# The last batch norm, residual and layer norm of a four-layer graph network in a written order: normalising on ScalarE, half of the residuals on TensorE, stores by GpSimd

## The chip, the cores and the metric

The kernel runs on one core of one Trainium2 chip. The metric is the device time of one execution in microseconds (us), the median of several runs. Engines: PE is TensorE's matmul, PEld its weight load, DVE is VectorE, ACT is ScalarE, POOL is GpSimd, SP is SyncE. A difference below 2% counts as "the same".

## The reference, cut to what matters

Four layers, each `x = layernorm(x + gnn_layer(x))`, on 128 batches of 128 nodes by 256 features. The change touches only the end of the last one:

```python
def _layernorm(x, axis=-1, eps=1e-5):
    m = jnp.mean(x, axis=axis, keepdims=True)
    v = jnp.var(x, axis=axis, keepdims=True)
    return (x - m) / jnp.sqrt(v + eps)

# layer 3
    x = agg.reshape(-1, d)
    h = jax.nn.relu(_batchnorm(x @ W1.T + b1, g1, be1))
    out = h @ W2.T + b2                  # "z product" below
    out = _batchnorm(out, g2, be2)       # "n2": needs all batches first
    return out.reshape(b, n, -1)
# ... cut
x = _layernorm(x + _L3_gnn_ref(x, adj, ...), axis=-1)   # "last part" below
```

A batch norm needs the moments of every batch, so the end falls into two stages with a full stop between them: the z product (with the first batch norm and relu applied on the way), then n2, the residual `x3` (the input of layer 3), the layer norm and the store.

## The kernel before

A group `q` is four batches (`QB`), and there are 32 groups (`NQ`). The result of the z product stays in SBUF as `agg`, features on partitions (128 x 512 for each half `o` of the 256 features). The last part scales and shifts it on ScalarE, transposes it on TensorE back to nodes on partitions, and VectorE does everything else.

```python
        for q in range(NQ):
            x3 = wk.tile([P, QB, D], F32, tag="x3", name=f"x3l{q}", bufs=7)
            nc.sync.dma_start(x3, x3_dram[q].rearrange("p (b d) -> p b d", b=QB))
            ag = outs[q]
            for o in range(DC):
                nc.scalar.activation(ag[:, o, :], ag[:, o, :], AF.Identity, bias=sh2[:, o:o + 1],
                                     scale=sc2[:, o:o + 1])
            for j in range(0, QB, 2):
                pt = ps("pt3").rearrange("p (b d) -> p b d", d=D)
                for t in range(2):
                    for o in range(DC):
                        nc.tensor.transpose(pt[:, t, o * P:(o + 1) * P], ag[:, o, (j + t) * N:(j + t + 1) * N], ident)
                nc.vector.tensor_add(x3[:, j:j + 2, :], x3[:, j:j + 2, :], pt)
                layer_norm(wk, x3[:, j:j + 2, :])
            nc.scalar.dma_start(out[q * QB:(q + 1) * QB].rearrange("b n d -> n b d"), x3)
```

`layer_norm` of two batches is, on VectorE, two `bn_stats`, two `bn_aggr`, a reciprocal and two `tensor_scalar` (subtract the mean, multiply), with one square root on ScalarE between them. No order is written down in this part: a scheduler places the instructions on each engine.

## Time and profile before

| what | before | how to read it |
|---|---|---|
| time | 3485.96 us (3485.91 to 3490.95, 3 runs) | the profiled run took 3485.64, its span is 3483.9 |
| first z load to first z matmul | 5.80 us (3112.19 to 3117.99) | timeline: issue by SP, then PE |
| z product on PE | 221.88 us | first matmul to end of the last |
| end of it to the first scaling | 3.39 us (3339.87 to 3343.26) | aggregating the moments and the small chain of n2 |
| last part | 140.6 us (3343.26 to 3483.9) | first scaling to the end of the span; 4.18 us for one group |

The lines that carry this are in the prediction. Two things of the timeline are not: what ScalarE does while VectorE is full, and who issues the stores.

```profile
3431.02 0.38 ACTq L749 DMA_DIRECT2D out_dram<-x3l  x1
...
3431.89 0.30 ACT L90 ACTIVATE ln_sd<-ln_mv,eps 128x2 f32<-128x2 f32 x1 [2.83 <-DVE ln_mv L85]
...
3479.96 0.38 ACTq L749 DMA_DIRECT2D out_dram<-x3l  x1
```

The columns are start, duration, engine, line, operation, and in brackets the idle time ahead of it with what ended it. Late in the part ScalarE has only the roots left and idles 2.83 us ahead of every second one. Its sequencer (ACTq) issues the stores at 0.38 us each; here that costs nothing, since ScalarE has time to spare. The last store is issued at 3479.96 and the program ends 3.9 us later.

### The profile page before, as it was taken

The page shows a single profiled execution, that of the slowest core. Times are in us where ns is not written, and L with a number is a line of the kernel's source. Part 1 is how long each engine was busy: PE and PEld are TensorE (multiplying, and loading weights), DVE is VectorE, ACT ScalarE, POOL GpSimd, SP SyncE. Part 2 cuts the span into 40 slices and gives each one's busy share as a digit, 9 for nine tenths or more (in the row PEclk, how much of TensorE's full clock was granted, in tenths as well). Part 3 has the DMA queues.
Part 4 walks back from the last instruction along what each step waited for, and adds up shares of the span by engine and source line. Part 5 has one row for each costly group of instructions (what it writes and reads, how often), then busy time and mean ns, then how long its engine had stood idle before and what let it go on. Part 6 is the DMA issues. An engine that isn't in the chain of part 4 may idle for free.

```text
span 3483.9 us, 33805 instructions
## 1 busy us (share of the span) xinstructions
PE 3303.1 (95%) x13130; PEld 2105.6 (60%) x13130; DVE 1797.1 (52%) x3549; ACT 974.6 (28%) x1637; POOL 543.6 (16%) x460
## 2 busy tenths in 40 slices
PE   5599999999999999999999999999999999989963
PEld 2366666666666666666666666666666666654442
DVE  6544455555554555554445554555545553233379
ACT  1122222222222222222222222222222222234452
POOL 3211111111111111111111111111111110000000
PEclk8799999999999999999999999999999999999975
DMA  6433333323222233333333323322233331034446
GB/s 201 120 86 97 85 97 97 97 79 97 89 83 74 83 91 98 97 98 97 91 92 97 97 82 94 93 82 78 75 91 97 97 91 37 19 123 173 157 132 224
DMA packets 127743, 347.78 MB, mean 100 GB/s; under 512 B 14432, under 2 KB 68576, under 8 KB 115040
## 3 DMA queue, kind: packets, MB, share of 16 engines
q0 software_dynamic: 40960, 135.29, 16.1%
q1 hardware_dynamic: 65168, 190.53, 15.3%
q10 hardware_dynamic: 21456, 19.81, 1.7%
q8 instruction: 104, 1.70, 0.2%
q14 instruction: 55, 0.45, 0.0%
HBM read 258.55 MB, written 87.03 MB: 99 GB/s over the span
## 4 chain that ended last, share of the span: by engine, by line
PE 91%; DVE 4%; DMA 2%; issue 1%; ACT 0%; POOL 0%; DVEq 0%; POOLq 0%; ACTq 0%; SPq 0%
PE ph L314 25%; PE p L325 13%; PE po L373 10%; PE po L728 6%; PE ph L412 6%; PE ph L294 6%; PE pq L167 6%; PE pm L304 3%; PE po L269 3%; PE pm L359 3%; PE py L260 2%; PE pa L398 2%; PE pm L280 2%; PE po L336 2%; DVE x3l L98 1%
## 5 line engine op out<-in xcount | busy, mean ns | idle before, releaser
L314 PE MATMUL ph<-m,w 128*128 128x512 f32 x2048 | 887.2, 594 | 3.9 <-DVE m L305 3.9
L314 PEld LDWEIGHTS ph<-m,w 128*128 128x128 f32 x2048 | 390.5, 191 | 481.6 <-issue 476.0
L325 PE MATMUL p<-w,h 128*128 128x256 f32 x2048 | 450.4, 381 | 0.0
L325 PEld LDWEIGHTS p<-w,h 128*128 128x128 f32 x2048 | 387.1, 190 | 52.2 <-issue 0.5
L180 POOL DMA_INDIRECT zs<-qd,src_idx x128 | 126.5, 989 | 1797.6 <-DVE f L214 1571.8
L373 PE MATMUL po<-l2w,ms 128*128 128x256 f32 x1536 | 347.6, 379 | 1.2 <-DVE ms L365 1.2
L317 ACT ACTIVATE h<-ph 128x512 f32<-128x512 f32 x256 | 152.8, 597 | 598.6 <-PE ph L314 598.6
L373 PEld LDWEIGHTS po<-l2w,ms 128*128 128x128 f32 x1536 | 284.6, 190 | 35.9 <-DVE ms L365 1.4
L294 PE MATMUL ph<-w,mx 128*128 128x512 f32 x512 | 235.7, 593 | 0.0
L167 PE MATMUL pq<-wqv,xt 128*128 128x512 f32 x512 | 231.1, 605 | 2.9 <-DVE xt L156 2.9
L728 PE MATMUL po<-zl,l3w 128*128 128x512 f32 x512 | 221.9, 597 | 10.5 <-ACT zl L723 10.5
L412 PE MATMUL ph<-ag,l3w 128*128 128x512 f32 x512 | 225.5, 593 | 0.3 <-ACT ag L401 0.3
L180 POOL DMA_INDIRECT zs<-qd,dst_idx x128 | 202.8, 1584 | 121.5 <-DMA zs<-qd,src_idx 101.4
L338 DVE TENSOR_TENSOR xr<-xr,po 128x512 f32<-128x512 f32 x64 | 43.7, 683 | 336.5 <-PE po L336 336.5
L90 ACT ACTIVATE ln_sd<-ln_mv,eps 128x2 f32<-128x2 f32 x256 | 75.4, 294 | 456.5 <-DVE ln_mv L85 449.9
L156 DVE COPY xt<-pt 128x512 f32<-128x512 f32 x64 | 41.4, 685 | 310.1 <-PE pt L154 310.0
L236 POOL DMA_INDIRECT attd<-at,att_idx x128 | 127.5, 996 | 440.4 <-DMA attd<-at,att_idx 283.4
L98 DVE TENSOR_SCALAR xr<-xr,ln_mv,ln_rs 128x256 f32<-128x256 f32 x384 | 179.7, 510 | 6.9
L728 PEld LDWEIGHTS po<-zl,l3w 128*128 128x128 f32 x512 | 98.1, 192 | 134.3 <-issue 112.2
L190 DVE SCALAR_TENSOR_TENSOR zs<-zs 128x1024 f32<-128x1024 f32 x128 | 155.6, 1216 | 35.2 <-DMA zs<-qd,dst_idx 35.2
L412 PEld LDWEIGHTS ph<-ag,l3w 128*128 128x128 f32 x512 | 96.9, 190 | 121.6 <-issue 112.3
L167 PEld LDWEIGHTS pq<-wqv,xt 128*128 128x128 f32 x512 | 97.2, 195 | 115.1 <-issue 110.4
(173 smaller groups left out, 3965.4 us busy)
## 6 DMA issues: line engine op xcount, KB each, us to landing
ad<-attd SPq DMA_DIRECT2D x32, 1024.0 KB, 4.7
zd<-z SPq DMA_DIRECT2D x32, 1024.0 KB, 7.3
zl<-zd SPq DMA_DIRECT2D x32, 1024.0 KB, 4.8
xg<-in_x_dram SPq DMA_DIRECT2D x32, 512.0 KB, 4.2
qd<-qt SPq DMA_DIRECT2D x32, 512.0 KB, 2.6
xr<-in_x_dram SPq DMA_DIRECT2D x32, 512.0 KB, 5.8
x3d<-xr SPq DMA_DIRECT2D x32, 512.0 KB, 2.9
x3l<-x3d SPq DMA_DIRECT2D x32, 512.0 KB, 4.4
```

Of the source, the lines that this page charges most:

```text
L98: nc.vector.tensor_scalar(r[:, i, :], r[:, i, :], mv[:, i, 0:1], rs[:, i:i + 1], op0=ALU.subtract, op1=ALU.mult)
L167: nc.tensor.matmul(pq, s.xts[i // 2][:, i % 2, c, :], wqv[:, c, :], start=(c == 0), stop=(c == DC - 1))
L180: nc.gpsimd.indirect_dma_start(out=s.z[c], out_offset=None, in_=s.qd, in_offset=bass.IndirectOffsetOnAxis(ap=idx[:, c:c + 1], axis=0), com ...
L190: nc.vector.scalar_tensor_tensor(z, z, SLOPE, z, op0=ALU.mult, op1=ALU.max)
L236: nc.gpsimd.indirect_dma_start(out=ad, out_offset=bass.IndirectOffsetOnAxis(ap=att_idx[:, c:c + 1], axis=0), in_=s.at[:, c, :], in_offset= ...
L294: nc.tensor.matmul(ph, s.mx[i // 2 * 2][:, i % 2, dc, :], w1_sb[:, dc, :], start=(dc == 0), stop=(dc == DC - 1))
L314: nc.tensor.matmul(ph, w2_sb[:, c, f * P:(f + 1) * P], s.m2[:, c].rearrange("p b n -> p (b n)"), start=(c == 0), stop=(c == K1 - 1))
L317: nc.scalar.activation(h.rearrange("p b n -> p (b n)"), ph, AF.Relu)
L325: nc.tensor.matmul(p3[:, t * D:(t + 1) * D], s.h2[f][:, j + t, :], w3_sb[:, f, :], start=(f == 0), stop=(f == K2 - 1))
L373: nc.tensor.matmul(po[:, i % 2, :], mss[i][:, t, dc, :], l2w[:, t, dc, :], start=(n3 == 0), stop=(n3 == 3 * DC - 1))
L412: nc.tensor.matmul(ph, l3w1[:, dc, c * P:(c + 1) * P], s.ag[:, dc, :], start=(dc == 0), stop=(dc == DC - 1))
L728: nc.tensor.matmul(po, w2t[:, c, o * P:(o + 1) * P], z[:, c, :], start=(c == 0), stop=(c == K3 - 1))
```

## The change

Intent: VectorE is the bound of the last part and ScalarE idles, so move the normalising to ScalarE (as `x * rs + nm` with `nm = -mean * rs`) and half of the residual adds to TensorE (a product by the identity that accumulates `x3` into the transposed result in PSUM). Normalise one group later than its moments, so that ScalarE doesn't wait for VectorE; one root serves four batches. Load up to 16 groups of `x3` into the buffers that z leaves. GpSimd issues the stores, so that ScalarE need not. Everything is in a written order, no scheduler.

```diff
-        for q in range(NQ):
-            x3 = wk.tile([P, QB, D], F32, tag="x3", name=f"x3l{q}", bufs=7)
 ... cut: the old loop, shown above; the z product is rewritten for two half loads of z
+        NB = 17
+        def buf(name):
+            return keep.tile([P, 2 * QB * N], F32, tag="buf", name=name, bufs=NB)
 ...
+        with tc.manual_schedule(engines=None):
 ... cut: z product and n2
+            def scaled(q):
+                ag = outs[q]
+                for o in range(DC):
+                    nc.scalar.activation(ag[:, o, :], ag[:, o, :], AF.Identity, bias=sh2[:, o:o + 1],
+                                         scale=sc2[:, o:o + 1])
+                pt = [ps("pt3").rearrange("p (b d) -> p b d", d=D) for _ in range(2)]
+                for j in range(QB):
+                    for o in range(DC):
+                        dst_ps, a_in = pt[j // 2][:, j % 2, o * P:(o + 1) * P], ag[:, o, j * N:(j + 1) * N]
+                        if j < 2:
+                            nc.tensor.transpose(dst_ps, a_in, ident)
+                        else:
+                            nc.tensor.matmul(dst_ps, a_in, ident, start=(j == 2 and o == 0), stop=False,
+                                             skip_group_check=True)
+                nc.tensor.matmul(pt[1], ident, x3s[q][:, 2:, :], start=False, stop=True, skip_group_check=True)
 ... cut: moments (add of the first half, bn_stats, bn_aggr) and coefficients (reciprocal, nm)
+            def apply(q):
+                rs, nm = coefs[q]
+                for i in range(QB):
+                    src_ = x3s[q][:, i, :] if i < 2 else sums[q][1][:, i - 2, :]
+                    nc.scalar.activation(x3s[q][:, i, :], src_, AF.Identity, bias=nm[:, i:i + 1], scale=rs[:, i:i + 1])
+                nc.gpsimd.dma_start(out[q * QB:(q + 1) * QB].rearrange("b n d -> n b d"), x3s[q])
+            for q in range(NB - 1):
+                load_x3(q)
+            scaled(0)
+            for q in range(NQ + 1):
+                if q < NQ:
+                    moments(q, 0)
+                if q + 1 < NQ:
+                    scaled(q + 1)
+                if q > 0:
+                    coefficients(q - 1)
+                    apply(q - 1)
+                    if q + NB - 2 < NQ:
+                        load_x3(q + NB - 2)
+                if q < NQ:
+                    moments(q, 1)
+                    sd = wk.tile([P, QB], F32, tag="sd3", name="sd3", bufs=2)
+                    nc.scalar.activation(sd, mvs[q][:, :, 1], AF.Sqrt, bias=eps)
+                    coefs[q] = sd
```

More of the change, by code (lines that the diff above doesn't have):

```diff
@@ L716, in gnn_stack @@
         sc1, sh1 = batch_norm(st1, K3, b1, g1, be1, "n1")
-        outs = []
-        for q in range(NQ):
-            z = wk.tile([P, K3, QB * N], F32, tag="zl", name="zl", bufs=4)
-            nc.sync.dma_start(z, z_dram[q].rearrange("p (c n) -> p c n", c=K3))
-            for c in range(K3):
-                nc.scalar.activation(z[:, c, :], z[:, c, :], AF.Relu, bias=sh1[:, c:c + 1], scale=sc1[:, c:c + 1])
-            ag = keep.tile([P, DC, QB * N], F32, tag=f"agg{q}", name=f"agg{q}")
-            for o in range(DC):
-                po = ps("po3")
-                for c in range(K3):
-                    nc.tensor.matmul(po, w2t[:, c, o * P:(o + 1) * P], z[:, c, :],
-                                     start=(c == 0), stop=(c == K3 - 1))
-                nc.vector.bn_stats(st2[:, o, q, :], po)
-                nc.vector.tensor_copy(ag[:, o, :], po)
-            outs.append(ag)
@@ L733, in gnn_stack @@
-        sc2, sh2 = batch_norm(st2, DC, b2, g2, be2, "n2")
-        for q in range(NQ):
-            x3 = wk.tile([P, QB, D], F32, tag="x3", name=f"x3l{q}", bufs=7)
-            nc.sync.dma_start(x3, x3_dram[q].rearrange("p (b d) -> p b d", b=QB))
-            ag = outs[q]
-            for o in range(DC):
-                nc.scalar.activation(ag[:, o, :], ag[:, o, :], AF.Identity, bias=sh2[:, o:o + 1],
-                                     scale=sc2[:, o:o + 1])
-            for j in range(0, QB, 2):
-                pt = ps("pt3").rearrange("p (b d) -> p b d", d=D)
-                for t in range(2):
-                    for o in range(DC):
-                        nc.tensor.transpose(pt[:, t, o * P:(o + 1) * P], ag[:, o, (j + t) * N:(j + t + 1) * N], ident)
-                nc.vector.tensor_add(x3[:, j:j + 2, :], x3[:, j:j + 2, :], pt)
-                layer_norm(wk, x3[:, j:j + 2, :])
-            nc.scalar.dma_start(out[q * QB:(q + 1) * QB].rearrange("b n d -> n b d"), x3)
+        NB = 17
@@ new lines, in buf, with load_z, load_x3, moments @@
+        def buf(name):
+            return keep.tile([P, 2 * QB * N], F32, tag="buf", name=name, bufs=NB)
+        def load_z(q):
+            z = [buf(f"zl{q}_{h}").rearrange("p (c n) -> p c n", c=2) for h in range(2)]
+            zq = z_dram[q].rearrange("p (c n) -> p c n", c=K3)
+            for h in range(2):
+                nc.sync.dma_start(z[h], zq[:, 2 * h:2 * h + 2, :])
+            return z
+        outs = []
+        with tc.manual_schedule(engines=None):
+            for q in range(NQ):
+                z = load_z(q)
+                for c in range(K3):
+                    zc = z[c // 2][:, c % 2, :]
+                    nc.scalar.activation(zc, zc, AF.Relu, bias=sh1[:, c:c + 1], scale=sc1[:, c:c + 1])
+                ag = keep.tile([P, DC, QB * N], F32, tag=f"agg{q}", name=f"agg{q}", bufs=1)
+                for o in range(DC):
+                    po = ps("po3")
+                    for c in range(K3):
+                        nc.tensor.matmul(po, w2t[:, c, o * P:(o + 1) * P], z[c // 2][:, c % 2, :],
+                                         start=(c == 0), stop=(c == K3 - 1))
+                    nc.vector.bn_stats(st2[:, o, q, :], po)
+                    nc.vector.tensor_copy(ag[:, o, :], po)
+                outs.append(ag)
+            sc2, sh2 = batch_norm(st2, DC, b2, g2, be2, "n2")
+            x3s, sums, mvs, coefs = {}, {}, {}, {}
+            def load_x3(q):
+                x3s[q] = buf(f"x3l{q}").rearrange("p (b d) -> p b d", b=QB)
+                nc.sync.dma_start(x3s[q], x3_dram[q].rearrange("p (b d) -> p b d", b=QB))
+            def scaled(q):
[5 more added lines that the diff above has]
+                for j in range(QB):
+                    for o in range(DC):
+                        dst_ps, a_in = pt[j // 2][:, j % 2, o * P:(o + 1) * P], ag[:, o, j * N:(j + 1) * N]
[5 more added lines that the diff above has]
+                nc.tensor.matmul(pt[1], ident, x3s[q][:, 2:, :], start=False, stop=True, skip_group_check=True)
+                sums[q] = pt
+            def moments(q, half):
+                if half == 0:
+                    mvs[q] = wk.tile([P, QB, 2], F32, tag="mv3", name="mv3", bufs=3)
+                    moments.st = wk.tile([P, QB, 6], F32, tag="st3", name="st3", bufs=2)
+                    nc.vector.tensor_add(x3s[q][:, :2, :], x3s[q][:, :2, :], sums[q][0])
+                src_ = x3s[q][:, :2, :] if half == 0 else sums[q][1]
+                for t in range(2):
+                    nc.vector.bn_stats(moments.st[:, 2 * half + t, :], src_[:, t, :])
+                for t in range(2):
+                    nc.vector.bn_aggr(mvs[q][:, 2 * half + t, :], moments.st[:, 2 * half + t, :])
+            def coefficients(q):
+                rs = wk.tile([P, QB], F32, tag="rs3", name="rs3", bufs=2)
+                nm = wk.tile([P, QB], F32, tag="nm3", name="nm3", bufs=2)
+                nc.vector.reciprocal(rs, coefs[q])
+                nc.vector.scalar_tensor_tensor(nm, mvs[q][:, :, 0], -1.0, rs, op0=ALU.mult, op1=ALU.mult)
+                coefs[q] = (rs, nm)
+            def apply(q):
[22 more added lines that the diff above has]
+                    coefs[q] = sd
```

## The prediction

> **What bounds the kernel now**
>
> I read the busy slices first, to find how much of the span the last part is.
>
> ```profile
> PE   5599999999999999999999999999999999989963
> DVE  6544455555554555554445554555545553233379
> ACT  1122222222222222222222222222222222234452
> PEclk8799999999999999999999999999999999999975
> ```
>
> One slice is 3483.9/40 = 87 us. TensorE (PE) fills every slice except the first and the last two. The change touches only code behind the big loop: the layer-3 product of stored z (slices 36 to 38), then the final batch norm, residual and layer norm (the last 1.6 slices), where PE drops to 6 and 3 tenths, VectorE (DVE) rises to 9 and the granted PE clock falls. The order of instructions of both kernels confirms that nothing ahead of that differs. So the ceiling is small: even an instant final part, 143 us, would be only 4.1%.
>
> Next the windows of that part (columns: stretch, length, busy time and count of PE, weight loads, DVE, ACT, POOL, then clock, DMA share, GB/s).
>
> ```profile
> 3341.00:3344.00 3.00, 0.00 (x0) 0.00 (x0) 2.05 (x8) 1.03 (x3) 0.00 (x0) 0.94 0.00 0
> 3360.00:3400.00 40.00, 19.00 (x79) 15.29 (x80) 40.00 (x153) 27.40 (x51) 0.00 (x0) 0.50 0.77 249
> 3420.00:3476.00 56.00, 19.41 (x80) 15.70 (x80) 56.00 (x216) 7.98 (x27) 0.00 (x0) 0.50 0.67 220
> ```
>
> DVE is busy all of the time; PE half of it or less, at half clock; ACT runs ahead with the scaling and then idles. DMA is high but not full. The chain of waits says the same with its period:
>
> ```profile
> 3428.01 0.57 DVE x3l L747
> 3428.58 0.09 DVE ln_mv L85
> 3428.67 0.57 DVE x3l L747
> 3429.24 0.14 DVE ln_rs L96 x2
> 3429.38 0.32 DVE ln_st L83
> 3429.70 1.28 DVE x3l L98 x4
> 3430.99 0.34 DVE ln_st L83
> 3431.32 0.08 DVE ln_mv L85
> 3431.40 0.31 DVE ln_st L83
> 3431.71 0.08 DVE ln_mv L85
> 3431.79 0.02 DVE ln_st L83
> 3431.81 0.20 issue
> 3432.01 0.17 DVE ln_mv L85
> 3432.19 0.57 DVE x3l L747
> ```
>
> From add to add 3432.19 - 3428.01 = 4.18 us: one group of four batches, nothing but DVE. Of it 1.28 are the four normalising instructions and 1.14 the two residual adds. 32 groups make 134 us of the 143. The groups of instructions of this window give the prices (busy time overlaps at the ends, so the chain's figures are the rates):
>
> ```profile
> L740 ACT ACTIVATE agg<-agg,n2shift,n2scale 128x512 f32<-128x512 f32 x64 | 47.5, 799 | 0.8 <-DVE n2shift L713 0.8
> L98 DVE TENSOR_SCALAR x3l<-x3l,ln_mv,ln_rs 128x256 f32<-128x256 f32 x128 | 44.4, 406 | 0.1
> L90 ACT ACTIVATE ln_sd<-ln_mv,eps 128x2 f32<-128x2 f32 x64 | 18.9, 295 | 71.2 <-DVE ln_mv L85 66.0 <-DVE ln_st L83 4.6 <-DVE ln_rs L96 0.2
> ```
>
> and one line of the timeline the rate of ACT back to back: seven in 5.05 us, that is (5.05 - 0.80)/6 = 0.71 each.
>
> ```profile
> 3343.26 5.05 ACT L740 ACTIVATE agg<-agg,n2shift,n2scale 128x512 f32<-128x512 f32 x7 [0.82 <-DVE n2shift L713]
> ```
>
> [...] The trace has only indirect GpSimd DMAs: 0.99 us of POOL for 128 rows, 1.58 with accumulation.
>
> [...]
>
> **The change part by part** (per group of four batches, "q")
>
> DVE. Removed: four tensor_scalar (-1.28), one of two adds (-0.57), one of two reciprocals (-0.07). Added: one tiny scalar_tensor_tensor for -mean/sd (+0.2, as the small chained operations of the batch norm are 0.2 apart). 4.18 - 1.92 + 0.2 = 2.46. The written order puts dependent operations next to each other (add then statistics, statistics then aggregate), some 0.25 more: about 2.7 us.
>
> ACT. Two scalings 2 x 0.71 = 1.42. Four normalising ACTIVATEs of 256 elements with two pointers[...]. One root for four instead of two for two: 0.295 - 0.09 = 0.2. Sum 3.55. Nothing gives ACT a rest, so ACT becomes the bound: 3.55, rounded to 3.6 for semaphores.
>
> PE. Eight transposes of a group took 1.94 us at half clock. Four stay, four become plain products by the identity[...], and the new 128x512 product adds the residual: 0.43 at full clock (221.9 us for 512), so 0.86 at half. About 3.1 us: below 3.6, near enough to watch.
>
> DMA. x3 for 16 groups is loaded into buffers that z leaves, during the z product, where queues have room (150 GB/s). Later a load and a store per group, 1 MB in 3.6 us = 290 GB/s; the loads are 15 groups ahead, so lateness costs nothing.
>
> Does the order close without waits? Count from ACT's root of q-1. It takes 0.2, the scalings of q+1 end at 1.6, and normalising q-1 wants its coefficients then. DVE's part for q starts when PE has the first half of q, about 1.0 after the scaling of q, so near -0.75; add, two statistics, aggregates and coefficients last some 1.95, done at 1.2. Slack 0.4. The second half is done near 2.1, the root wants it at 3.4. So ACT should run without holes.
>
> Start and end. First apply: scaling of 0 ends 1.5, first half 2.5, moments to 5.1, root, scaling of 2 to 6.9, coefficients: 7.2 us after the first scaling. Then 29 groups x 3.6 = 104.4. The last two have no scaling before them but expose root and coefficients: 2.8 + 2.85, and 2.0 for the last apply: 7.65. The last store through GpSimd:[...] about 5 (3.9 now). 7.2 + 104.4 + 7.65 + 5 = 124.3, against 3483.9 - 3343.3 = 140.6 now. Gain 16.3.
>
> The z product. It is 222 us of PE before and after. Its first load is cut in two halves, so ACT can begin after 512 KB: the 1 MB load took 4.83 us, so PE starts some 1.4 earlier. In exchange the batch norm between the parts is in written order: one of the two 0.93 us aggregations no longer runs early, and mean and shift no longer beside the root: +1.3. Net -0.1.
>
> Sum: 3485.96 - 16.3 - 0.1 = 3469.5.
>
> **The rivals**
>
> GpSimd becomes the bound. A store has 512 rows of 1 KB; if generation scales from the 128-row gather (0.94 plus a 0.3 gap), it is up to 5 us a group and the part is 32 x 5 = 160 plus ends, time near 3515. Against it: accumulation adds 0.6 us[...], which is 4.7 ns a row, so 512 rows are some 3 us with the fixed part, hidden below 3.6. A seventh of my belief, mostly with a mild excess (4 us, near 3483).
>
> ACT pays more for waits. If instructions behind semaphores lose the 0.09 overlap, seven of them add 0.6 us, T = 4.2, and nothing is gained: 3488. Against it: the ACTIVATEs of the z product wait on DMA and PE semaphores and still come every 0.71 (16 in 11.38).
>
> PE becomes the bound, if half-clock products cost 0.4 each: 3.6 to 3.7, hardly a change: 3472. If the fuller PE earns the full clock, it is half that, and ACT still bounds.
>
> DVE stays the bound through stalls: it would need 1.5 us of them to reach 4.18. I give it little.
>
> **Range and chances**
>
> Most weight on T from 3.45 to 3.75, which is 3465 to 3474. The tails are longer upward. Range 3459 to 3486. Faster by 2% would need 70 us, half of the last part: T below 1.9, less than ACT's instructions take. Slower by 2% needs T above 6.2. Both 0.01 to 0.02.
>
> **What would show it**
>
> Right: in the last part ACT near 100% busy, DVE near 75%, chain of waits on the normalising and scaling lines of ACT, 3.5 to 3.7 us from one root to the next; normalising 0.57 to 0.59 us each; PE about 3 us a group; POOL below ACT; the last store landing some 5 us after the last apply; the first z product some 1.4 us earlier. Wrong: holes in ACT with DVE coefficients or a GpSimd store as releaser, POOL above 3.6 us a group, or PE as what moments wait for.

ScalarE's 3.55 us came to 1.42 for the scalings, 1.93 for the four normalisings (the 2.8, 2.85 and 2.0 at the end use it too) and 0.2 for the root; the 0.09 taken off is the overlap, 0.80 - 0.71. An estimate from the trace of before comes near: 0.71 for 512 elements, less the 0.219 by which a copy of 512 outlasts one of 256 (585 against 366 ns, lines L361 and L168), is 0.49 for each, 1.96 for four. TensorE's 3.1 held 0.97 for four transposes, 0.86 for the residual product and the estimate for four plain products. The last store's 5 us had three terms; it is the author's estimate. The forecast came to 3485.96 - 16.3 - 0.1 = 3469.5.

## The result, and the profile after

The changed kernel took 3470.46 us (3467.67 to 3474.1, four runs), the kernel before 3486.15 in the four runs of the same rounds: ratio 0.9952, 95% interval 0.9935 to 0.9970, "the same". Ratios here are the mean time of one kernel's runs over that of the other's of the same rounds, so not quite the ratio of the medians. The profiled run is the 3474.1 one; everything ahead of the change is 4.9 us longer in it than in the profiled run of before (first z load at 3117.07, not 3112.19) with the same instructions (no run tells why), so I count from that load on:

| stretch (us) | before | after | difference | predicted |
|---|---|---|---|---|
| first z load to first z matmul | 5.80 | 5.03 | -0.8 | -1.4 |
| z product on PE | 221.88 | 222.55 | +0.7 | 0 |
| end of it to the first scaling | 3.39 | 4.54 | +1.2 | +1.3 |
| last part | 140.6 | 122.9 | -17.7 | -16.3 |
| sum | 371.7 | 355.0 | -16.7 | -16.4 |

The busy slices first, as in the prediction:

```profile
PE   5599999999999999999999999999999999989986
DVE  6544555555555555544555555555555444223357
ACT  1122222222222222222222222222222222216439
PEclk7799999999999999999999999999999999999999
```

At the end ACT stands at 9 where DVE did, DVE has fallen to 7, and PE's clock no longer falls. The windows (stretch, length, PE, weight loads, DVE, ACT, POOL, clock, DMA share, GB/s) say it in numbers:

```profile
3344.00:3360.00 16.00, 10.32 (x44) 6.82 (x42) 10.42 (x33) 6.82 (x12) 0.00 (x0) 0.79 0.20 65
3360.00:3400.00 40.00, 29.42 (x156) 17.86 (x155) 32.00 (x130) 40.00 (x82) 9.15 (x12) 1.00 0.79 269
3400.00:3440.00 40.00, 30.44 (x166) 19.19 (x167) 31.45 (x124) 40.00 (x82) 8.30 (x11) 1.00 0.65 231
```

ACT is busy in all of the 40 us, DVE in 79 to 80%, PE in 74 to 76% at full clock (before: half clock), POOL in 21 to 23%. One group in the timeline shows the period and the prices:

```profile
3419.17 0.40 ACT L813 ACTIVATE sd<-mv,eps 128x4 f32<-128x4 f32 x1
3419.36 1.62 ACT L758 ACTIVATE agg<-agg,n2shift,n2scale 128x512 f32<-128x512 f32 x2
...
3419.68 0.75 POOL L795 DMA_DIRECT2D out_dram<-x3l  x1 [2.73 <-DVE st L779]
...
3420.76 1.20 ACT L794 ACTIVATE x3l<-x3l,nm,rs 128x256 f32<-128x256 f32 x2
...
3421.42 1.06 PE L767 MATMUL pt<-ident,agg 128*128 128x128 f32 x8
3421.61 0.69 DVE L776 TENSOR_TENSOR x3l<-x3l,pt 128x512 f32<-128x512 f32 x1 [0.65 <-PE pt L765]
3421.75 1.12 ACT L794 ACTIVATE x3l<-pt,nm,rs 128x256 f32<-128x256 f32 x2
...
3422.31 1.02 PE L769 MATMUL pt<-x3l,ident 128*128 128x512 f32 x2
...
3422.65 0.41 ACT L813 ACTIVATE sd<-mv,eps 128x4 f32<-128x4 f32 x1
3422.84 0.93 ACT L758 ACTIVATE agg<-agg,n2shift,n2scale 128x512 f32<-128x512 f32 x1
```

From scaling to scaling 3422.84 - 3419.36 = 3.48 us: root, two scalings, four normalisings, no idle time in brackets on any ACT line. By their starts, the root takes 0.19, the two scalings 1.40, the first two normalisings 0.99, the other two 0.90. A store holds POOL for 0.75 us. Two MATMUL records stand on L769 although the source has one product there: a float32 product leaves two records here, and by their starts the eight records of L767 (four products) took 0.89.

The groups of instructions of the last part hold a trap for reading:

```profile
L758 ACT ACTIVATE agg<-agg,n2shift,n2scale 128x512 f32<-128x512 f32 x64 | 50.9, 890 | 1.1 <-DVE n2shift L713 1.1
L794 ACT ACTIVATE x3l<-x3l,nm,rs 128x256 f32<-128x256 f32 x64 | 37.4, 677 | 1.3 <-DVE nm L787 1.3
L794 ACT ACTIVATE x3l<-pt,nm,rs 128x256 f32<-128x256 f32 x64 | 34.9, 639 | 0.0
L795 POOL DMA_DIRECT2D out_dram<-x3l x32 | 24.2, 757 | 355.9 <-DVE nm L787 273.3 <-DVE st L779 65.6 <-DVE mv L781 10.5
```

The scaling is the same instruction as before, but its mean is 890 ns, not 799. It did not get slower: at the start of the part a pair lasts 1.50 in the timeline, later up to 1.70, while the period stays 3.48. Here the recorded durations of ScalarE, which has no rest, stretch and overlap more. The rate (start to start) held at 3.48, the mean did not hold at 799. The chain of waits has the same rhythm:

```profile
3405.44 0.19 ACT sd L813
3405.62 1.41 ACT agg L758 x2
3407.03 0.04 ACT x3l L794
3407.07 0.13 issue
3407.20 0.02 ACTq L794
3407.22 0.12 issue
3407.34 1.58 ACT x3l L794 x3
3408.92 0.19 ACT sd L813
3409.11 1.41 ACT agg L758 x2
```

Nothing but ACT lines stands in it, 3.48 us from root to root, with small "issue" pieces in which it waited for nothing that the profile shows.

Start and end of the part, on ACT and POOL:

```profile
3349.19 2.93 ACT L758 ACTIVATE agg<-agg,n2shift,n2scale 128x512 f32<-128x512 f32 x4 [1.09 <-DVE n2shift L713]
3356.13 0.30 ACT L813 ACTIVATE sd<-mv,eps 128x4 f32<-128x4 f32 x1 [4.01 <-DVE mv L781]
3356.33 1.50 ACT L758 ACTIVATE agg<-agg,n2shift,n2scale 128x512 f32<-128x512 f32 x2
3358.11 1.09 ACT L794 ACTIVATE x3l<-x3l,nm,rs 128x256 f32<-128x256 f32 x2 [0.28 <-DVE nm L787]
...
3466.87 0.75 POOL L795 DMA_DIRECT2D out_dram<-x3l  x1 [1.87 <-ACT x3l L794]
```

The first normalising comes 8.9 us after the first scaling: ACT waits 4.01 us for the first moments. The last store is issued at 3466.87 and the program ends at 3472.1, 5.2 us later.

### The profile page after: what moved, and what is told of

Read it like the earlier page. It is cut to its first block, busy times and chain, and to the rows that moved or that the text cites. A ratio compares the mean times of both kernels' runs of the same rounds, so it can differ in the third digit from the quotient of the medians.

```text
span 3472.1 us, 34279 instructions
## 1 busy us (share of the span) xinstructions
PE 3336.4 (96%) x13322; PEld 2112.7 (61%) x13322; DVE 1752.8 (50%) x3389; ACT 1024.6 (30%) x1733; POOL 564.9 (16%) x492
## 3 DMA queue, kind: packets, MB, share of 16 engines
q0 software_dynamic: 45568, 152.07, 17.7%
## 4 chain that ended last, share of the span: by engine, by line
PE 91%; issue 2%; ACT 2%; DVE 1%; DMA 1%; POOL 0%; POOLq 0%; ACTq 0%; SPq 0%; DVEq 0%
PE ph L314 25%; PE p L325 13%; PE po L373 10%; PE po L741 6%; PE ph L412 6%; PE ph L294 6%; PE pq L167 6%; PE pm L304 3%; PE po L269 3%; PE pm L359 3%; PE py L260 2%; PE pa L398 2%; PE pm L280 2%; PE po L336 2%; ACT x3l L794 1%
## 5 line engine op out<-in xcount | busy, mean ns | idle before, releaser
L90 ACT ACTIVATE ln_sd<-ln_mv,eps 128x2 f32<-128x2 f32 x192 | 56.4, 294 | 386.2 <-DVE ln_mv L85 384.8
```

## The experiments

Twelve kernels ran, in three jobs on three chips. There the kernel before took 3530.9 to 3538.1 us, about 1.4% more than in the first comparison. The difference lies ahead of the last part, which begins between 3385 and 3397 in these profiles and not near 3349; why, no run tells, and each kernel is compared with the runs of before of its own job. All gave the reference's result. In the texts, theory A is the author's own account (in most of them, that ScalarE's instructions set the period of the changed last part) and B its rival; each text says both.

| kernel | ratio to before | 95% | last part, us | period of a group, us |
|---|---|---|---|---|
| changed kernel (control) | 0.9942 | 0.9925 to 0.9958 | 122.9 | 3.48 |
| both residual adds on VectorE | 0.9957 | 0.9941 to 0.9974 | 124.6 | 3.57 |
| stores issued by ScalarE | 0.9999 | 0.9982 to 1.0015 | 139.2 | 4.05 |
| stores issued by SyncE | 0.9935 | 0.9918 to 0.9952 | 121.3 | 3.48 |
| no written order | 0.9943 | 0.9926 to 0.9960 | 120.0 | 3.48 |
| 9 buffers, not 17 | 0.9952 | 0.9936 to 0.9969 | 122.9 | 3.48 |
| before, with normalising on ScalarE only | 1.0064 | 1.0047 to 1.0081 | 162.4 | 5.06 |
| a quarter of the normalising on VectorE | 0.9933 | 0.9916 to 0.9949 | 113.9 | 3.19 |
| half of the normalising on GpSimd | 0.9896 | 0.9880 to 0.9913 | 100.8 | 2.75 |
| the same, no written order | 0.9858 | 0.9841 to 0.9874 | 93.0 | 2.50 |
| scaling by TensorE, one-row shift | 1.0202 | 1.0165 to 1.0238 | 219.3 from n2's root | 6.7 to 6.8 in its middle |
| scaling by TensorE, 128-row shift | 1.0038 | 1.0018 to 1.0058 | 154.7 from n2's root | 4.36 |

"Last part" is from the first scaling to the end of the span. The last two have no scaling on ScalarE and are counted from the root of n2, which is 1.38 us ahead of the first scaling in the written order.

**The control.** The changed kernel itself, in the third job.

> The changed kernel itself, unedited, as a control on the chip of these runs. Theory A (the chip matters only ahead of the last part): ratio to the kernel before 0.995 as in the first result, the last part 122.9 us from the first scaling to the end. Rival B (the slower chip has another last part too): more than 1 us away from that.

Ratio 0.9942 (3517.91 against 3538.05), and the last part is 122.9 us (3397.22 to 3520.1), as in the first profile to the tenth. The slower chip does not touch it, and the nine-buffer kernel below, on another of the three, has 122.9 too, so last parts may be compared across jobs.

**Both residual adds on VectorE.** The TensorE part of the change is undone:

```diff
-                        if j < 2:
-                            nc.tensor.transpose(dst_ps, a_in, ident)
-                        else:
-                            nc.tensor.matmul(dst_ps, a_in, ident, start=(j == 2 and o == 0), stop=False, ...)
-                nc.tensor.matmul(pt[1], ident, x3s[q][:, 2:, :], start=False, stop=True, skip_group_check=True)
+                        nc.tensor.transpose(dst_ps, a_in, ident)
 ...
-                    nc.vector.tensor_add(x3s[q][:, :2, :], x3s[q][:, :2, :], sums[q][0])
+                xh = x3s[q][:, 2 * half:2 * half + 2, :]
+                nc.vector.tensor_add(xh, xh, sums[q][half])
```

> The changed kernel with both residual adds on VectorE again (plain transposes on TensorE, all four normalisations from SBUF). Theory A (ScalarE sets the pace of the last part, 3.48 us a group in the changed kernel): ScalarE's work is the same, VectorE grows from 2.8 by 0.57 to 0.7 to about 3.45 and just fits, so 3.5 to 3.75 us a group and at most 9 us slower than the changed kernel: 3470 to 3480. Rival B (the residual on TensorE is what brought the gain, VectorE is what counts): back near 4 us a group, 3484 or more.

3519.74 against 3533.83, last part 124.6: only 1.7 us longer than the control. The window of its middle:

```profile
3440.00:3480.00 40.00, 24.55 (x89) 16.93 (x89) 38.47 (x138) 40.00 (x80) 8.94 (x12) 0.50 0.68 236
```

ACT is still busy all of the time; DVE rises to 96% and stays just below it. So the residual on TensorE takes work from an engine that still had room for it. It is worth 1.7 us. The period is 3.57 (roots at 3439.71 and 3443.27), 0.09 over the control's 3.48, and that is what ScalarE saves there by normalising two batches from PSUM rather than SBUF (0.90 against 0.99 for two): even this small gain is one of ScalarE's time. The clock is a second finding: with transposes alone PE is 61% busy and stays at 0.50.

**Stores issued by ScalarE.** One word:

```diff
-                nc.gpsimd.dma_start(out[q * QB:(q + 1) * QB].rearrange("b n d -> n b d"), x3s[q])
+                nc.scalar.dma_start(out[q * QB:(q + 1) * QB].rearrange("b n d -> n b d"), x3s[q])
```

> The changed kernel with the stores issued by ScalarE, as before. Theory A (ScalarE has no hole, so 0.38 us of issue for each store adds to its group): 3.8 to 3.9 us a group, 32 x 0.38 = 12 us slower than the changed kernel, about 3482. Rival B (issuing runs beside the arithmetic, the sequencer is ahead of the engine): 3.48 us a group, and the last store lands about 1 us sooner: 3469.

3533.89 against 3533.83: the whole gain is gone. Last part 139.2, 16.3 us longer than the control (12 were expected). Its timeline on ACT, and its window:

```profile
3475.21 1.00 ACT L794 ACTIVATE x3l<-pt,nm,rs 128x256 f32<-128x256 f32 x2
3476.23 0.38 ACTq L795 DMA_DIRECT2D out_dram<-x3l  x1
3476.66 0.30 ACT L813 ACTIVATE sd<-mv,eps 128x4 f32<-128x4 f32 x1 [0.46 <-DVE mv L781]
3476.86 0.80 ACT L758 ACTIVATE agg<-agg,n2shift,n2scale 128x512 f32<-128x512 f32 x1
```

```profile
3440.00:3480.00 40.00, 25.56 (x139) 16.12 (x140) 28.17 (x107) 35.62 (x70) 0.00 (x0) 1.00 0.71 225
```

The profile puts the hole of 0.46 us down to VectorE's moments. But the moments that this root needs were done at 3474.21 in the same timeline; those that end just ahead of it are the next group's. The line above it tells better: the issue can start only when the last normalising has ended (3475.21 + 1.00), holds ScalarE's sequencer for 0.38, and the root starts right after. With the overlap of some 0.1 us that back-to-back instructions have (a scaling lasts 0.80 and the next starts after 0.71) and these two lose, that is the 0.57 us between the periods 4.05 and 3.48. Over 32 groups it is 18 us, about the gain of the change; the stores by SyncE below confirm it.

**Stores issued by SyncE.** The same line with `nc.sync.dma_start`.

> The changed kernel with the stores issued by SyncE instead of GpSimd. Theory A (all that counts is that ScalarE doesn't issue them): 3.48 us a group; the last store lands about 1.3 us sooner, as the 3.9 us of the kernel before against 5.2 say: last part about 121.5 us. Rival B (loads behind stores in one order hold each other up): x3 loads late, 125 us or more.

3515.09 against 3538.05, last part 121.3, period 3.48. It need not be GpSimd; of the three that were tried only ScalarE lengthens the period (4.05, not 3.48). The 1.6 us less than in the control lie at the end: the last normalising starts 116.4 us after the first scaling in both (3510.84 - 3394.48, 3513.57 - 3397.22), and from there to the end of the span it is 5.0 us here, 6.5 in the control.

**No written order.** The scheduler orders the same instructions:

```diff
-        with tc.manual_schedule(engines=None):
+        with ExitStack():
```

> The changed kernel without the written order: the scheduler orders the z product and the last part. Theory A (only ScalarE's sum of work counts): the same 3.48 us a group on the mean, 3467 to 3474, though scalings run ahead. Rival B (the order is needed): holes in ScalarE while it waits for coefficients, 3.7 us a group or more, 3478 or more.

3514.98 against 3533.83; last part 120.0, same period. The start differs:

```profile
3395.53 7.86 ACT L758 ACTIVATE agg<-agg,n2shift,n2scale 128x512 f32<-128x512 f32 x11 [0.82 <-DVE n2shift L713]
```

Eleven scalings run while PE and VectorE prepare the first group, where the written order makes ScalarE wait 4.01 us after four. So the written order does not gain here; in the profiles it costs 2.9 us in this part. In the whole times that is within the intervals.

**Nine buffers.** `NB = 9` in place of 17: eight groups of x3 ahead, not sixteen.

> The changed kernel with 9 buffers instead of 17 for z and x3, so x3 is 8 groups ahead and not 16. Theory A (loads are hidden anyway: a load and a store per group are 1 MB in 3.48 us, 300 GB/s, and 310 GB/s were seen in the run without the written order): the last part, from the first scaling to the end, stays at 123 to 125 us. Rival B (the 16 groups loaded ahead are what keeps it fed): it grows by 5 us or more, with x3 loads as what the additions wait for.

3513.01 against 3530.93, last part 122.9.

```profile
3428.00:3468.00 40.00, 29.85 (x161) 18.48 (x162) 31.46 (x127) 40.00 (x81) 8.72 (x12) 1.00 0.88 306
```

More of the loads fall into this stretch (306 GB/s, not some 231 to 269), and ACT still has no hole. Loading sixteen ahead brings nothing over eight.

**Before, with the normalising on ScalarE and nothing else.**

```diff
-                layer_norm(wk, x3[:, j:j + 2, :])
+                xj = x3[:, j:j + 2, :]
+                mv = norm_stats(wk, xj)
+                sd = norm_root(wk, mv)
+                ... rs = 1/sd, nm = -mean*rs on VectorE
+                for t in range(2):
+                    nc.scalar.activation(xj[:, t, :], xj[:, t, :], AF.Identity, bias=nm[:, t:t + 1], scale=rs[:, t:t + 1])
```

> The kernel before with one part of the change: normalisation on ScalarE, all else as before (scheduler's order, pairs of batches, both adds on VectorE, stores by ScalarE). By the sum of ScalarE: 2 x 0.71 + 4 x 0.49 + 2 x 0.2 = 3.8 us, with 0.38 of store issue 4.2; VectorE 4.18 - 1.28 + 0.4 = 3.3. Theory A (ScalarE's sum, issue included, sets the pace): about 4.2 us a group, no gain, 3482 to 3490. Rival B (issue is free): 3.8 us, 3474 to 3477.

3555.77 against 3533.83: slower, by 0.64%, and slower than theory A had it (in the steady middle three groups take 15.18 us, 5.06 each, where 4.2 was expected). Its window and, from the waits of its last part, one line (in total, times, longest, in us):

```profile
3440.00:3480.00 40.00, 14.77 (x58) 10.53 (x58) 26.09 (x111) 30.83 (x65) 0.00 (x0) 0.54 0.66 210
```

```profile
ACT x3l L756 <- DVE ln_nm L754: 20.1, 19, 2.1
```

Neither engine is full (VectorE 65%, ScalarE 77%): they hand two batches back and forth, root to reciprocal to normalising, and wait for each other. Here the store stands on ScalarE too. So the move that gives VectorE its time back loses alone; it gains with what the change sets around it. The stores account for 16.3 us, the difference of the ScalarE stores to the control. Some 21 us more (162.4 - 139.2, less 1.7 for the residual) lie between this kernel and the one with ScalarE stores; normalising a group later and one root for four are what mainly differs there, but no run isolates them, so that split is worked out and not shown.

**A quarter of the normalising back on VectorE**, which has a fifth of its time free:

```diff
-                for i in range(QB):
+                nc.vector.tensor_scalar(x3s[q][:, 0, :], x3s[q][:, 0, :], rs[:, 0:1], nm[:, 0:1], op0=ALU.mult, op1=ALU.add)
+                for i in range(1, QB):
```

> The changed kernel with one of the four normalisations of a group on VectorE again. Theory A (ScalarE bounds with no hole): ScalarE 3.48 - 0.49 = 3.0, VectorE 2.8 + 0.33 = 3.1, so 3.1 to 3.2 us a group and the last part 111 to 114 us instead of 123. Rival B (it is the chain through all engines that sets 3.48, not ScalarE alone): the same 123 or longer.

3506.42 against 3530.93, last part 113.9, period 3.19, ACT and DVE both at 97%. Taking one normalising from ScalarE shortens the period, as its being the bound demands.

**Half of the normalising on GpSimd**, which was 22% busy:

```diff
+                    if i < 2:
+                        nc.gpsimd.tensor_scalar(x3s[q][:, i, :], src_, rs[:, i:i + 1], nm[:, i:i + 1], op0=ALU.mult, op1=ALU.add)
+                    else:
+                        nc.scalar.activation(...)
```

> The changed kernel with the two normalisations that read SBUF on GpSimd (0.75 us a group busy, all of it store issue). ScalarE 3.48 - 0.98 = 2.5, VectorE 2.8, TensorE 2.65, GpSimd 0.75 + 2 x 0.6 (an estimate: an addition of 512 elements lasted 1.27 there) = 2.0. Theory A: VectorE becomes the bound, 2.8 to 3.0 us a group, last part 102 to 108 us. Rival B (GpSimd's normalisation is slow[...]): 3.3 us or more a group.

3492.49 against 3530.93, last part 100.8, period 2.75 (roots at 3430.59 and 3433.34).

```profile
3429.00:3449.00 20.00, 17.20 (x100) 11.31 (x99) 19.48 (x83) 18.81 (x36) 13.40 (x22) 1.00 1.00 369
```

A normalising takes 545 ns in the mean on GpSimd (406 on VectorE in the kernel before). Now DVE is the fullest at 97%, with ACT at 94%, and the DMA engines are in use all of the time (share 1.00); no run isolates which of them sets 2.75.

**The same without the written order.** Both edits together.

> Two normalisations on GpSimd as before in these runs (100.8 us of last part, 2.75 us a group), without the written order. Theory A (leaving the order to the scheduler gains its 3 us at the start here too): 97 to 99 us. Rival B (with VectorE as the bound and the DMA queues full, the scheduler's order makes holes): 102 us or more.

3486.84 against 3538.05: ratio 0.9858, and below the control of the same job (3517.91). Last part 93.0, better than expected, period 2.50.

```profile
3426.00:3446.00 20.00, 19.80 (x118) 13.93 (x116) 19.52 (x89) 20.00 (x42) 15.75 (x26) 1.00 1.01 385
```

PE, DVE, ACT and the DMA engines are all above 97%. This version is faster than both kernels, clear of the noise, though by less than the 2% that count. Here the scheduler's order is worth 7.8 us, over twice what it was with the period at 3.48.

**The scaling on TensorE.** ScalarE drops the scaling; the identity becomes a diagonal matrix of `sc2`, and the shift comes from a product with one row of contraction:

```diff
-                    nc.scalar.activation(ag[:, o, :], ag[:, o, :], AF.Identity, bias=sh2[:, o:o + 1], scale=sc2[:, o:o + 1])
+                        nc.tensor.matmul(dst_ps, a_in, dg[:, o, :], start=(j % 2 == 0 and o == 0), stop=False, ...)
+                    if j % 2:
+                        nc.tensor.matmul(pt[j // 2], one, shr, start=False, stop=(j == 1), ...)   # one: 1 x 128, shr: 1 x 512
```

(Also `NB = 16`, for the room that the new tiles take.)

> The changed kernel with the scaling taken from ScalarE: the transposing products multiply by a diagonal matrix of the scales, and the shift is added by a product of a row of ones with the row of shifts (16 buffers for space). ScalarE has 2.1 us a group left, VectorE 2.8. Theory A (a float32 product of 512 columns costs [...]0.87 us at full clock, one of 128 columns 0.22, as the trace after shows): TensorE has 8 x 0.22 + 3 x 0.87 = 4.4 us a group and becomes the bound, last part near 150 us. Rival B (the prices of the prediction, 0.43[...]): 2.4 us of TensorE, VectorE bounds at 2.8 to 3.0, last part near 105 us.

3609.04 against 3530.93 (3585.15 to 3610.63): ratio 1.0202, its interval on both sides of 2%. The direction is theory A's (ScalarE freed, TensorE the bound), the size is larger.

```profile
3468.00:3488.00 20.00, 20.00 (x67) 11.65 (x66) 8.37 (x32) 6.84 (x15) 2.26 (x3) 0.74 0.49 157
```

PE is busy all of the time and is yet granted 0.74 of its clock in the mean: it goes back and forth between 0.50 and 1.00. Later in the same part there are stretches at 1.00 (3565 to 3588, for one), in which a group takes 5.14. The suspects are the one-row products, two in each group.

**The same with 128 rows.** `one` is 128 x 128 of 1/128 and `shr` has 128 equal rows; the same sum, and nothing else changes in the loop.

> The diagonal-matrix kernel (last part 219 us, 6.7 us a group with TensorE always busy but at a mean clock of 0.75) with the shift added by a product that uses all 128 rows (ones/128 times the shifts in every row) and not one row. Theory A (the clock falls because a product that fills one row counts as little activity): clock 1.00, 5.1 us a group as in its stretches at full clock, last part 165 to 180 us. Rival B (it falls for another reason, as the mixed small products): clock 0.75 as before, 210 us or more.

3551.25 against 3538.05 (two runs), shorter than expected.

```profile
3429.00:3449.00 20.00, 20.00 (x102) 13.31 (x101) 13.13 (x53) 10.52 (x24) 3.01 (x4) 1.00 0.76 242
```

The clock is 1.00 and a group takes 4.36 us, not 6.7. So it was the single row: here products that fill one of 128 rows kept the engine busy in the profile (100%) but did not hold its clock (0.74 in the mean); why, no run tells. They also cost more by themselves: 5.14 against 4.36 us a group where both have the full clock (a one-row product 1.05 us from start to start, a 128-row one 0.86). With 128 rows at full clock TensorE still takes 4.36 us against ScalarE's 3.48, and the idea loses either way.

## Why the prediction was right, point by point

**ScalarE becomes the bound: right.** ACT 100% busy, DVE 79 to 80% (75 expected), the chain on ACT alone. Experiments confirm it from both sides: what loads ScalarE (a store issue) lengthens the period, what relieves it (a normalising on VectorE or GpSimd) shortens it, and what relieves VectorE alone (the residual) moves next to nothing. The sum of 3.55 was 3.48; taking 3.6 for semaphores was too careful, they cost nothing visible (no idle time on any ACT line of the group above). One sign of being right needs care: "normalising 0.57 to 0.59 us each" fits the start of the part (two from SBUF in 1.09, at 0.50 apart), not the means of 677 and 639 ns, for the reason given above.

**VectorE's 2.7 us a group: right.** 31.45 of 40 times 3.48 is 2.74. The 0.25 in it for dependent neighbours was the author's estimate; one part can be read: the statistics that follow their own add start 0.70 us after it (3356.01 to 3356.71), where 0.57 passed from an add to the next instruction before.

**The last part: 124.3 predicted, 122.9 measured**, with two errors of opposite sign inside. The first normalising came 8.9 us after the first scaling, not 7.2. The prediction had the first moments done at 5.1; they were done at 6.9, where the root starts (3356.13). The trace after shows what they waited for, in its chain and on VectorE:

```profile
3351.66 1.71 PE pt L767 x8
3353.37 1.72 PE pt L769 x2
3355.11 0.76 DVE L779 BATCH_NORM_STATS2 st<-pt 128x6 f32<-128x256 f32 x2 [1.72 <-PE pt L769]
```

These are the four plain products and the residual product of the first group. They take twice the 0.89 and 0.87 of later, since the clock is still 0.50 (3351 to 3355); so the late start is TensorE's price, which the next point is about. The stretch from there to the last store was 108.8 (3358.11 to 3466.87), not 112.05, for the period. The store's end of 5.2 was as expected (5), but the trace of before, with 3.9 for a store by ScalarE, doesn't show the terms given for it, so that hit is partly luck. So is a median within 1 us of the forecast: the four runs alone spread over 6.4 us.

**TensorE was mis-sized by half, and a second error hid it.** The term "0.43 at full clock" came from 221.9 us for 512, read as 512 products. They are 256 products with two records each, so the product costs 0.87 at full clock, and each plain 128-column product two records as well (four in 0.89). At the half clock that the prediction assumed, the group would take 2 x 0.89 + 2 x 0.87 + 0.97 (four transposes, half of the 1.94 for eight) = 4.5 us. TensorE would then have been the bound, above the 4.18 of before. It did not happen, except in the first group, since the clock rose to 1.00, which the prediction had only as a possibility in a rival. So "TensorE below ScalarE" came true by luck, not by the sum.

**Why the clock rose** is not isolated by a run. One reading is that the plain products raised it. At first sight the runs agree: with transposes alone and PE 61% busy the clock is 0.50, with half of them plain products and PE 64% busy (the ScalarE stores) it is 1.00. But the trace of the kernel before, which has only transposes (`nc.tensor.transpose`) there, does not. At the start of its last part PE ran 42 of them without a break (8.32 us from 3344.13), and the clock rose:

```profile
3345.00:3350.00 5.00, 5.00 (x24) 4.94 (x25) 4.23 (x15) 5.00 (x9) 0.00 (x0) 0.50 0.00 0
3351.00:3357.00 6.00, 3.79 (x26) 2.49 (x24) 6.00 (x23) 4.93 (x9) 0.00 (x0) 1.00 0.50 177
```

The changed kernel rose in the same way: PE busy without a break at 0.50 from 3351 to 3355, at 1.00 from 3356 on. A reading that fits these two traces, and that no run isolates, is that work without a break raised the clock. The eight transposes of a group at half clock take 2.2 us of the 3.57 with both adds on VectorE, so PE has a break in every group; the changed kernel's group at half clock is estimated at 4.5 us (above), more than the period of 3.48, so it has none. The kernel with one-row products doesn't fit it: PE busy all of the time, at a mean of 0.74. The shares of 61 and 64% were read at different clocks and can't be compared.

**GpSimd: the rival's 3 us was mis-sized.** A store of 512 rows held POOL 0.75 us. The estimate from the accumulating gathers (1.58 us against 0.99 for 128 rows, taken as 4.7 ns a row, though no trace shows single rows) does not carry to a plain store. It was to be hidden and was, so nothing followed from it.

**The half load: -1.4 predicted, -0.8 measured.** How the 1.4 came from the 4.83 us of the whole load is not said; half of the bytes took 4.16 us from the issue to the first relu, where all took 4.93. **The written n2: +1.3 predicted, +1.2 measured.** The z product grew by 0.7, taken as 0.

**Parts of the change.** The gain needs the normalising on ScalarE, stores kept off ScalarE, and something of the rest: with the first alone the kernel was slower, and some 21 us of that are not the stores (normalising a group later, one root for four; not isolated). The prediction priced the first two moves right but, like the change, took the parts as one. By themselves the residual on TensorE is worth 1.7 us, loading sixteen ahead nothing over eight, GpSimd nothing over SyncE, and the written order costs some 3 us in the profiles. "Faster by 2%" was excluded since it needs a period under 1.9; even the best version, at 2.50, stays at 1.4%.

## What to carry to other kernels

When a change moves work from a full engine to an idle one, add up all that the receiver does, store issues too: 0.38 us of issuing per group on the new bound took back all of the gain. Count float32 products by the source and not by the records (two each here), price TensorE at both clocks that the traces show (0.50 and 1.00), and look at which of them the trace grants, at the start of a stage too. Stop when several engines meet near full, and look for one with nothing to do: here it was GpSimd, and its share took the gain from 0.6% to 1.0%.
